# A mixture-of-experts kernel: an expert's last tile of at most 64 tokens in 32-column groups

## The chip, the cores and the metric

The kernel runs on one core of a Trainium2 chip. The metric is device time in microseconds of one execution. A core has five engines with instruction queues of their own: TensorE (PE) multiplies matrices into PSUM, VectorE (DVE) and ScalarE (ACT) read PSUM and work elementwise, GpSimd (POOL) issues the indirect DMAs here, and SyncE (SP) issues nearly all other DMAs. [...]

## What is computed

x has 4 sequences of 512 tokens with 256 features. The reference adds two layers to it, each on top of a small conditioned layer:

```python
x = x + attn(cond(x, cond_8))            # attention, 16 heads of 16 features, keys and values shared
x = x + ffn(cond2(x, cond_8))            # the mixture of experts, 8 experts

# in ffn: 8 groups of 256 tokens
probs = softmax(xg @ w_router)           # over 8 experts
_, idx = top_k(probs, 2)                 # two experts for each token
# at most 128 tokens of a group are kept for one expert
h = gelu(expert_in @ wi[e])              # 256 -> 1024
expert_out = h @ wo[e]                   # 1024 -> 256
out = sum over the two experts of expert_out * probs
```

All is float32. How many tokens an expert gets depends on the data and is known only on the chip.

## The kernel before

The first 380 us or so are the conditioned layer and the attention, with the routing of each finished sequence worked in beside it. The matter here is the last part, the experts.

**Rows by expert.** Every routed token row (256 features and 8 extra numbers: token number, first expert, two shares) is scattered by an indirect DMA (L654) into a DRAM buffer `xp`, where each expert has a range of 1024 rows and its rows lie without gaps. Behind the last row of an expert lie zero rows.

**Units.** The experts' work is cut into units. A double unit is 256 rows of one expert, a single is 128 rows. Unit numbers stand for slots of lists: NA = 6 doubles that are listed early, from the first sequences; NB = 5 doubles from all rows; then NTILE slots for singles, everything that is left. `list_of` (L835) computes on VectorE, for each slot, its expert (`texp`, and the weights' row in `table`) and its first row (`table`). It is called for the early doubles, then in `lists_of_rest` (L877) for the later doubles and for the singles, in this order; `count` (L887) holds the number of singles. Slots past the end of a list point to zero rows. A partly filled single costs what a full one does.

**A unit's steps.** `fetch_in` and `fetch_out` (L901, L907) read a row number from `table` into a register of SP and load 1 MB each of the expert's weights wi and wo (L896); the tiles have three buffers each. `fetch_rows` (L913) loads the rows (L918, four buffers). `turn` (L954) transposes the rows on TensorE (L960; four transposes for a double, two for a single) and VectorE copies them to SBUF (L962). `up` (L964) multiplies with wi: for each of 8 blocks of 128 hidden features two matmuls (L975) with a 128 x 128 block of wi as the stationary operand and the unit's 128 or 256 tokens moving; ScalarE applies Gelu from PSUM (L979). `put` (L1001) multiplies with wo for each 128 tokens: 8 matmuls with 128 tokens stationary and 256 output features moving (L1005). `share` (L986) finds each row's weight and target on VectorE (L994 to L998), VectorE scales the result into `y` (L1015), POOL casts the target row (L1013) and issues an indirect DMA that adds `y` to the output (L1016). The adds of a unit wait for the adds of the unit before, because the same rows may be hit.

**The order** is written out by hand in `run` (L1107), without a scheduler. Step k: load the rows of unit k+2; `up` of unit k; load wi for k+3; `turn` of unit k+1; `put` of unit k-1; load wo for k+2. `place` (between these steps) puts in what is left of the last sequence's attention and routing; its twelfth entry is `lists_of_rest`. Units run in this order: the 6 early doubles, NSURE = 14 singles, the 5 later doubles. Then `count` is loaded, and only if it is over 14 do further singles run in a branch.

Parts used below: an f32 matmul shows as two records in the trace. The attention weighs values in `weigh` (L421): four matmuls, each with 32 stationary columns, write the four groups of 32 partitions of one PSUM bank.

Of the kernel before, what the change touches and what calls it, by code (L numbers as in the profile page):

```python
# [10 lines left out]
F32 = mybir.dt.float32  # L11
I32 = mybir.dt.int32
AF = mybir.ActivationFunctionType
ALU = mybir.AluOpType
# [8 lines left out]
NE = 8  # L23
# [7 lines left out]
NCH = NT // P  # L31
EROWS = NG * CAP
NTILE = 2 * NCH + NE - 1


N0, NA, NB, NSURE, NNEXT = 2, 6, 5, 14, 18
XROW = D + NE
WROW = 1024 + 10

# [2 lines left out]
def adaln_attn_ffn_kernel(  # L42
# [32 lines left out]
    def bank(tag):  # L75
        return ps.tile([P, 512], F32, tag=tag, name=f"ps_{tag}", bufs=BANKS[tag])
# [731 lines left out]

    NUNIT = NA + NB + NTILE
    pairs = fp.tile([P, NE + 1], F32, name="pairs", bufs=1)
    nc.gpsimd.memset(pairs, 0.0)
    texp = fp.tile([P, NUNIT], F32, name="texp", bufs=1)
# [3 lines left out]
    def of_experts(t, less, op, begin):  # L818

        n = begin.shape[2]  # L820
        cmp = fp.tile([P, NE, NG], F32, name="cmp", bufs=1)[:, :, 0:n]
        nc.vector.scalar_tensor_tensor(
            cmp, free.unsqueeze(2).to_broadcast([P, NE, n]), less, begin, ALU.add, op
        )
        nc.vector.tensor_reduce(t, cmp, AX.X, ALU.add)

    def ends_of_experts(t):

        cmp = fp.tile([P, NE, NE], F32, name="cmp2", bufs=1)
        nc.vector.tensor_tensor(cmp, through, t.unsqueeze(1).to_broadcast([P, NE, NE]), ALU.mult)  # L830
        end = fp.tile([P, NE], F32, name="end", bufs=1)
        nc.vector.tensor_reduce(end, cmp, AX.X, ALU.add)
        return end

    def list_of(u0, n, got, end, used, width):  # L835


        step = fp.tile([P, NE], F32, name="step", bufs=1)
        nc.vector.tensor_tensor(step, used[:, 1 : NE + 1], used[:, 0:NE], ALU.subtract)
        nc.vector.tensor_tensor(step, step, got, ALU.subtract)  # L840
        nc.vector.tensor_scalar(step, step, float(EROWS // (width * P)), None, ALU.add)
        past = fp.tile([P, NTILE, NE], F32, name="past", bufs=1)[:, 0:n]
        nc.vector.tensor_tensor(
            past, tilen[:, 0:n].unsqueeze(2).to_broadcast([P, n, NE]),
            end.unsqueeze(1).to_broadcast([P, n, NE]), ALU.is_ge,
        )
        te = texp[:, u0 : u0 + n]
        nc.vector.tensor_reduce(te, past, AX.X, ALU.add)
        nc.vector.tensor_scalar(
            table[:, 1, u0 : u0 + n], te, float(NE - 1), 4.0 * P, ALU.min, ALU.mult  # L850
        )
        nc.vector.tensor_tensor(past, past, step.unsqueeze(1).to_broadcast([P, n, NE]), ALU.mult)
        row = fp.tile([P, NTILE], F32, name="trow", bufs=1)[:, 0:n]
        nc.vector.tensor_reduce(row, past, AX.X, ALU.add)
        nc.vector.scalar_tensor_tensor(row, row, used[:, 0:1], tilen[:, 0:n], ALU.add, ALU.add)
        nc.vector.tensor_scalar(
            table[:, 0, u0 : u0 + n], row, float(NE * EROWS // (width * P)), float(width * P),
            ALU.min, ALU.mult,
        )
# [17 lines left out]
    def lists_of_rest():  # L877
        for _ in list_of_pairs(NA, NB):
            pass
        got = fp.tile([P, NE], F32, name="got", bufs=1)  # L880
        twice = fp.tile([P, NE + 1], F32, name="twice", bufs=1)
        nc.vector.tensor_scalar(twice, pairs, 2.0, None, ALU.mult)
        of_experts(got, 0.0, ALU.is_gt, begin)
        nc.vector.tensor_tensor(got, got, twice[:, 0:NE], ALU.subtract)
        end = ends_of_experts(got)
        list_of(NA + NB, NTILE, got, end, twice, 1)
        nc.vector.tensor_copy(count, end[:, NE - 1 : NE])  # L887

    wi_of, wo_of, xt_of, xT_of, hT_of = {}, {}, {}, {}, {}
    reg, adds, now = {}, [], []  # L890
# [1 line left out]
    def width(u):  # L892
        return 2 if u < NA + NB else 1
# [60 lines left out]
    def turn(u, tag="a"):  # L954
# [6 lines left out]
        xT_of[u] = fp.tile([P, 2, 2 * P], F32, name="xT")[:, :, 0 : w * P]  # L961
        nc.vector.tensor_copy(xT_of[u], pt)  # L962

    def up(u, half):  # L964

        n = width(u) * P
        if half == 0:
            t = ep.tile([P, 4, 4, P], F32, name="e").rearrange("p a b t -> p (a b t)")
            hT_of[u] = t[:, 0 : F // P * n].rearrange("p (f t) -> p f t", f=F // P)
        each = 512 // n  # L970
        for f0 in range(4 * half, 4 * half + 4, each):
            ph = bank("m")
            for k in range(each):
                for c in range(2):
                    mm(  # L975
                        ph[:, ts(k, n)], wi_of[u][:, c, ts(f0 + k, P)], xT_of[u][:, c, :],
                        start=c == 0, stop=c == 1,
                    )
            nc.scalar.activation(  # L979
                hT_of[u][:, f0 : f0 + each].rearrange("p f t -> p (f t)"), ph,  # L980
                AF.Gelu_apprx_tanh,
            )
# [17 lines left out]

    def put(u, h):  # L1001

        po = bank("x")
        for fc in range(F // P):
            mm(  # L1005
                po[:, 0:D], hT_of[u][:, fc, ts(h, P)], wo_of[u][:, fc, :],
                start=fc == 0, stop=fc == F // P - 1,
            )
        if h == 0:
            share(u)  # L1010
        w0, at = shares[u]
        to = fp.tile([P, 1], I32, name="to_row", bufs=6)
        nc.gpsimd.tensor_copy(to, at[:, h : h + 1])  # L1013
        y = fp.tile([P, D], F32, name="y", bufs=6)
        nc.vector.tensor_scalar(y, po[:, 0:D], w0[:, h : h + 1], None, ALU.mult)  # L1015
        i = nc.gpsimd.indirect_dma_start(  # L1016
            out=out_rows,
            out_offset=bass.IndirectOffsetOnAxis(ap=to, axis=0),
            in_=y,
            in_offset=None,  # L1020
            compute_op=ALU.add,
        )


        for k in adds[-1] if adds else ():
            tc.add_manual_dep(i.ins, k.ins.name, AFTER, reason="same rows")
        if h > 0:
            tc.declare_no_dep(i.ins, group=f"unit{u}", reason="other tokens")
        tc.add_to_no_dep_group(f"unit{u}", i.ins)
        if u < NA:  # L1030
            tc.declare_no_dep(i.ins, group="last rows", reason="other sequences")
            tc.add_to_no_dep_group("early adds", i.ins)
        elif u == first_of_rest[0] and h == 0:
            for k in last_rows:
                tc.add_manual_dep(i.ins, k.ins.name, AFTER, reason="rows of the last sequence")
        now.append(i)
        if h == width(u) - 1:
            adds.append(list(now))
            now.clear()
# [46 lines left out]
    def place():  # L1086

        for name in final.get(next(places), ()):
            if name == "rest":
                lists_of_rest()  # L1090
                ready.update(range(NA, NUNIT))
                for f, u in late:
                    f(u)
                late.clear()
            else:
                work[B - 1][name]()
# [10 lines left out]
    def run(units, rows, begun=False):  # L1107

        if not begun:
            turn(units[0])  # L1110
        for k in range(len(units) + 1):
            for u in units[k : k + 1]:
                for x in rows(k):
                    fetch_rows(units[x])
                if begun and k == 0:
                    turn(units[1], "x")
                else:
                    up(u, 0)
                if width(u) == 2:
                    place()  # L1120
                up(u, 1)
                for x in units[k + 3 : k + 4]:
                    fetch(fetch_in, x)
                for x in units[k + 1 : k + 2]:
                    if not begun or k > 0:
                        turn(x)
                place()
            for u in units[k - 1 : k] if k else ():
                for h in range(width(u)):
                    put(u, h)  # L1130
                    place()
            for x in units[k + 2 : k + 3]:
                fetch(fetch_out, x)

    singles = range(NA + NB, NUNIT)
    units = [*range(NA), *singles[:NSURE], *range(NA, NA + NB)]

    def rows_behind(k):
        return (k + 2,) if k + 2 < len(units) else ()

    run(units, rows_behind, begun=True)
    filled = nc.values_load(count[0:1, 0:1], min_val=0, max_val=NTILE)

    def more(units):
        for u in units[:3]:
            fetch_in(u)
            fetch_out(u)
        for u in units[:2]:
            fetch_rows(u)
        run(units, lambda k: range(k + 2, len(units))[:1])  # L1150

    with tc.If(filled > NSURE):
        more(singles[NSURE:NNEXT])
        with tc.If(filled > NNEXT):
            more(singles[NNEXT:])


# [78 lines left out]
```

## Time and profile before

| | |
|---|---|
| three runs | 663.63 us median (662.09 to 665.27) |
| the profiled execution | 663.3 us, its span 661.6 us, mean granted clock 0.991 |
| TensorE busy | 642.0 us |
| VectorE, ScalarE, GpSimd busy | 324.2, 226.0, 111.6 us |
| DMA | 107.46 MB, mean 162 GB/s |
| first up of an expert unit, last down | 380.4 us, 647.9 us |
| matmul records of up (L975), down (L1005) | 800, 576 |
| row adds (L1016) | 36, 6.2 us from issue to landing |

The span runs from the first to the last instruction; the device time has 1.7 us more. The page gives each engine's busy time, the chain of waits that ended last, and the costliest groups of instructions: line, engine, operation, output and inputs, partitions x elements, count, busy time, mean duration. In the timeline a line holds start, duration, engine, line, operation and how many records were merged; in brackets the idle time before it and what ended it. Matmuls overlap, so the distance of two starts tells more than a duration.

### The profile page before, as it was taken

The page shows a single profiled execution, that of the slowest core. Times are in us where ns is not written, and L with a number is a line of the kernel's source. Part 1 is how long each engine was busy: PE and PEld are TensorE (multiplying, and loading weights), DVE is VectorE, ACT ScalarE, POOL GpSimd, SP SyncE. Part 2 cuts the span into 40 slices and gives each one's busy share as a digit, 9 for nine tenths or more (in the row PEclk, how much of TensorE's full clock was granted, in tenths as well). Part 3 has the DMA queues.
Part 4 walks back from the last instruction along what each step waited for, and adds up shares of the span by engine and source line. Part 5 has one row for each costly group of instructions (what it writes and reads, how often), then busy time and mean ns, then how long its engine had stood idle before and what let it go on. Part 6 is the DMA issues. An engine that isn't in the chain of part 4 may idle for free.

```text
span 661.6 us, 10602 instructions
## 1 busy us (share of the span) xinstructions
PE 642.0 (97%) x3988; PEld 393.3 (59%) x3988; DVE 324.2 (49%) x782; ACT 226.0 (34%) x400; POOL 111.6 (17%) x146
## 2 busy tenths in 40 slices
PE   8999999999999999999999899999999999999991
PEld 3444454333334433343344388888999999988881
DVE  1184745577667687867887625472122222221210
ACT  1122123566665465546545631311012111121110
POOL 1600000000000000400040402245322222222231
PEclk9999999999999999999999899999999999999997
DMA  7943971200232114320144399429899999974411
GB/s 234 371 137 95 317 224 49 81 33 18 63 99 84 34 33 131 132 65 17 46 139 152 102 390 273 138 83 297 238 297 303 340 334 319 348 224 121 88 18 26
DMA packets 65724, 107.46 MB, mean 162 GB/s; under 512 B 6914, under 2 KB 27266, under 8 KB 65666
## 3 DMA queue, kind: packets, MB, share of 16 engines
q1 hardware_dynamic: 50066, 87.96, 40.3%
q0 software_dynamic: 6720, 9.05, 7.2%
q10 hardware_dynamic: 8880, 9.71, 4.7%
q8 instruction: 33, 0.54, 0.3%
q14 instruction: 25, 0.20, 0.1%
HBM read 79.59 MB, written 26.98 MB: 161 GB/s over the span
## 4 chain that ended last, share of the span: by engine, by line
PE 88%; DMA 6%; DVE 3%; issue 1%; SPq 1%; POOL 0%; POOLq 0%; DVEq 0%
PE ps_m L374 19%; PE ps_x L1005 17%; PE ps_m L975 16%; PE ps_a L421 10%; PE ps_x L262 4%; PE ps_a L278 4%; PE ps_x L280 4%; PE ps_x L533 2%; PE ps_x L312 2%; PE ps_x L403 2%; PE ps_x L501 2%; DMA wo_sb<-in_wo_dram 2%; DMA inv<-od 1%; PE ps_x L327 1%; PE ps_a L960 1%
## 5 line engine op out<-in xcount | busy, mean ns | idle before, releaser
L378 DVE TENSOR_REDUCE negm<-ps_m 128x1 f32<-128x512 f32 x250 | 160.5, 684 | 64.9 <-PE ps_x L403 43.8
L407 ACT ACTIVATE e<-ps_x 128x512 f32<-128x512 f32 x244 | 132.4, 594 | 107.9 <-PE ps_x L403 101.4
L374 PE MATMUL ps_m<-k,q 32*128 32x512 f32 x500 | 152.3, 639 | 0.4 <-DVE negm L378 0.4
L403 PE MATMUL ps_x<-q,k 32*128 32x512 f32 x488 | 139.6, 642 | 1.9 <-DMA q<-nmT 1.9
L975 PE MATMUL ps_m<-xT,wi_sb 128*128 128x128 f32 (+1 forms) x800 | 130.3, 321 | 0.0
L1005 PE MATMUL ps_x<-wo_sb,e 128*128 128x256 f32 x576 | 128.5, 379 | 0.0
L975 PEld LDWEIGHTS ps_m<-xT,wi_sb 128*128 128x128 f32 x800 | 118.9, 191 | 10.1 <-issue 0.4
L1005 PEld LDWEIGHTS ps_x<-wo_sb,e 128*128 128x128 f32 x576 | 107.6, 190 | 13.7
L979 ACT ACTIVATE e<-ps_m 128x512 f32<-128x512 f32 x72 | 42.8, 597 | 194.3 <-PE ps_m L975 192.8
L374 PEld LDWEIGHTS ps_m<-k,q 32*128 32x128 f32 x500 | 46.5, 183 | 55.7 <-DVE negm L378 25.4
L1016 POOL DMA_INDIRECT out_dram<-y,to_row x36 | 56.1, 1558 | 131.6 <-DVE y L1015 33.2
L421 PE MATMUL ps_a<-e,v 128*32 128x256 f32 x1024 | 76.6, 392 | 0.1
L421 PEld LDWEIGHTS ps_a<-e,v 128*32 128x32 f32 x1024 | 23.3, 109 | 80.2 <-issue 66.5
L962 DVE COPY xT<-ps_a 128x256 f32<-128x256 f32 (+1 forms) x23 | 12.2, 529 | 95.1 <-PE ps_a L960 95.1
L1015 DVE TENSOR_SCALAR y<-ps_x,w 128x256 f32<-128x256 f32 x36 | 17.4, 482 | 81.5 <-PE ps_x L1005 81.5
L654 POOL DMA_INDIRECT xp<-x,to_i x32 | 32.9, 1028 | 53.7 <-DVE negm L378 28.8
L403 PEld LDWEIGHTS ps_x<-q,k 32*128 32x128 f32 x488 | 38.2, 184 | 4.4 <-issue 4.2
L583 POOL TENSOR_SCALAR x<-mk 128x4 f32<-128x4 f32 x4 | 0.8, 196 | 208.0 <-DVE mk L580 208.0
L283 DVE SCALAR_TENSOR_TENSOR hid<-ps_x,wo_sb,sg 128x512 f32<-128x512 f32 x16 | 12.0, 749 | 45.5 <-PE ps_x L280 45.5
L278 PE MATMUL ps_a<-xT_sb,wi_sb 128*128 128x512 f32 x64 | 30.5, 599 | 0.3 <-DMA wi_sb<-in_wcond_dram 0.3
L280 PE MATMUL ps_x<-xT_sb,wi_sb 128*128 128x512 f32 x64 | 30.1, 592 | 0.0
L1013 POOL CAST to_row<-at 128x1 int32<-128x1 f32 x36 | 20.1, 558 | 55.1 <-DVE at L998 55.1
(150 smaller groups left out, 436.9 us busy)
## 6 DMA issues: line engine op xcount, KB each, us to landing
wi_sb<-in_wi_dram SPq DMA_DIRECT2D x25, 1024.0 KB
wo_sb<-in_wo_dram SPq DMA_DIRECT2D x25, 1024.0 KB
xp<-zeros ACTq DMA_DIRECT2D x1, 8712.0 KB
q<-qd SPq DMA_DIRECT2D x8, 512.0 KB
wi_sb<-in_wcond_dram SPq DMA_DIRECT2D x15, 256.0 KB
od<-stage SPq DMA_DIRECT2D x15, 256.0 KB
xt<-xp SPq DMA_DIRECT2D x11, 264.0 KB
wo_sb<-in_wcond_dram SPq DMA_DIRECT2D x4, 517.0 KB
```

What stands on the lines that cost most here:

```text
L278: mm(pu, wu[:, c, :], xT_sb[:, c, ts(b, T)], start=c == 0, stop=c == 1)
L280: mm(pg, wg[:, c, :], xT_sb[:, c, ts(b, T)], start=c == 0, stop=c == 1)
L374: mm(pm, q[32 * j : 32 * j + 32, i, ts(hg, P)], k[32 * j : 32 * j + 32, :], start=True, stop=True,)
L378: nc.vector.tensor_reduce(nm[:, i, j : j + 1], pm, AX.X, ALU.max, negate=True)
L403: mm(px, k[rows_j, ts(sc, P)], seqs[u // 4]["q"][rows_j, :, ts(u % 4, P)], start=True, stop=True,)
L407: nc.scalar.activation(e_of[n][:, :, j, :].rearrange("p h (i t) -> p i h t", i=4), px.rearrange("p (i h t) -> p i h t", i=4, h=4), AF.Exp,)
L421: i = mm(pa_of[u][32 * hh : 32 * hh + 32, j0 * P : (j0 + nj) * P], seqs[b]["v"][:, sc, :], e[:, hh, j0 : j0 + nj].rearrange("p j n -> p (j ...
L654: i = nc.gpsimd.indirect_dma_start(out=xp, out_offset=bass.IndirectOffsetOnAxis(ap=s["to_i"][:, k, ch : ch + 1], axis=0), in_=s["x3"][:, c ...
L975: mm(ph[:, ts(k, n)], wi_of[u][:, c, ts(f0 + k, P)], xT_of[u][:, c, :], start=c == 0, stop=c == 1,)
L979: nc.scalar.activation(hT_of[u][:, f0 : f0 + each].rearrange("p f t -> p (f t)"), ph, AF.Gelu_apprx_tanh,)
L1005: mm(po[:, 0:D], hT_of[u][:, fc, ts(h, P)], wo_of[u][:, fc, :], start=fc == 0, stop=fc == F // P - 1,)
L1016: i = nc.gpsimd.indirect_dma_start(out=out_rows, out_offset=bass.IndirectOffsetOnAxis(ap=to, axis=0), in_=y, in_offset=None, compute_op=AL ...
```

## The change

`lists_of_rest` now makes two lists of what the doubles leave: tiles with more than 64 rows (slots as before) and, behind them, one slot per expert for a last tile of 1 to 64 rows. NSURE goes from 14 to 10, and NSMALL = 4 slots of the new list run without a branch. `count` becomes the largest excess of the two lists over 10 and 4; if it is over 0, the branch runs further units of both kinds.

A small unit takes the same row load, `turn`, two weight loads and row add. In between it differs. `up_small` makes 32 tokens the stationary operand and 512 columns of wi the moving one: four matmuls (two halves of the 64 tokens, two halves of the 1024 hidden features) write the four groups of 32 partitions of one bank, twice for the 256 input features; one Gelu follows. `turn_small` transposes the 128 x 512 result in four blocks, and VectorE copies it. `put_small` makes 16 matmuls with 32 stationary columns and 256 moving ones; two partition groups hold the sum of one half of the hidden features, two that of the other. ScalarE copies one half out of PSUM, VectorE adds the other, and scales. 64 rows are added to the output.

In the order, a small unit's `turn_small` stands after the `put` of the unit before it. The 5 later doubles and the 4 small units alternate, beginning and ending with a double.

```diff
-N0, NA, NB, NSURE, NNEXT = 2, 6, 5, 14, 18
+HALF = 64
+N0, NA, NB, NSURE, NNEXT, NSMALL = 2, 6, 5, 10, 18, 4
...
-    NUNIT = NA + NB + NTILE
+    NUNIT = NA + NB + NTILE + NE
...
-        of_experts(got, 0.0, ALU.is_gt, begin)
-        nc.vector.tensor_tensor(got, got, twice[:, 0:NE], ALU.subtract)
-        end = ends_of_experts(got)
-        list_of(NA + NB, NTILE, got, end, twice, 1)
-        nc.vector.tensor_copy(count, end[:, NE - 1 : NE])
+        most = fp.tile([P, 1], F32, name="most", bufs=1)
+        nc.vector.memset(most, 0.0)
+        for u0, n, less, sure in (
+            (NA + NB, NTILE, -float(HALF), NSURE), (NA + NB + NTILE, NE, 0.0, NSMALL)
+        ):
+            of_experts(got, less, ALU.is_gt, begin)
+            nc.vector.tensor_tensor(got, got, twice[:, 0:NE], ALU.subtract)
+            end = ends_of_experts(got)
+            list_of(u0, n, got, end, twice, 1)
+            nc.vector.tensor_tensor(twice[:, 0:NE], twice[:, 0:NE], got, ALU.add)
+            nc.vector.scalar_tensor_tensor(
+                most, end[:, NE - 1 : NE], -float(sure), most, ALU.add, ALU.max
+            )
+        nc.vector.tensor_copy(count, most)
...
+    def up_small(u):
+        t = ep.tile([P, 4, 4, P], F32, name="e").rearrange("p a b t -> p (a b t)")
+        hT_of[u] = t
+        ph = bank("m")
+        for c in range(2):
+            for n in range(4):
+                mm(
+                    ph[32 * n : 32 * n + 32, :], xT_of[u][:, c, ts(n % 2, 32)],
+                    wi_of[u][:, c, ts(n // 2, 512)], start=c == 0, stop=c == 1,
+                )
+        nc.scalar.activation(t[:, 0:512], ph, AF.Gelu_apprx_tanh)
+
+    def turn_small(u):
+        t = hT_of[u]
+        pt = bank("x")
+        for k in range(4):
+            nc.tensor.transpose(pt[:, ts(k, P)], t[:, ts(k, P)], ident)
+        nc.vector.tensor_copy(t[:, 512:1024], pt)
+
+    def put_small(u):
+        hT = hT_of[u][:, 512:1024].rearrange("p (k t) -> p k t", k=4)
+        po = bank("x")
+        for k in range(4):
+            for n in range(4):
+                mm(
+                    po[32 * n : 32 * n + 32, 0:D], hT[:, k, ts(n, 32)],
+                    wo_of[u][:, 4 * (n // 2) + k, :], start=k == 0, stop=k == 3,
+                )
+        share(u)
...
+        nc.scalar.copy(half, po[HALF:P, 0:D])
+        nc.vector.tensor_tensor(y[0:HALF], po[0:HALF, 0:D], half, ALU.add)
+        nc.vector.tensor_scalar(y[0:HALF], y[0:HALF], w0[0:HALF], None, ALU.mult)
+        add(u, to[0:HALF], y[0:HALF], 0)
...
+            for u in units[k : k + 1]:
+                if is_small(u):
+                    turn_small(u)
...
-    units = [*range(NA), *singles[:NSURE], *range(NA, NA + NB)]
+    units = [*range(NA), *singles[:NSURE]]
+    for n in range(max(NB, NSMALL)):
+        units += [*range(NA, NA + NB)[n : n + 1], *small[:NSMALL][n : n + 1]]
...
-    with tc.If(filled > NSURE):
-        more(singles[NSURE:NNEXT])
+    with tc.If(left > 0):
+        more([*singles[NSURE:NNEXT], *small[NSMALL:]])
```

More of the change, by code (lines that the diff above doesn't have):

```diff
@@ L962, in turn, with is_small @@
         nc.vector.tensor_copy(xT_of[u], pt)
+    def is_small(u):
+        return u >= NA + NB + NTILE
+    def up_small(u):
[25 more added lines that the diff above has]
+        share(u)
+        w0, at = shares[u]
+        to = fp.tile([P, 1], I32, name="to_row", bufs=6)
+        nc.gpsimd.tensor_copy(to, at[:, 0:1])
+        y = fp.tile([P, D], F32, name="y", bufs=6)
+        half = fp.tile([HALF, D], F32, name="half", bufs=2)
+        nc.scalar.copy(half, po[HALF:P, 0:D])
+        nc.vector.tensor_tensor(y[0:HALF], po[0:HALF, 0:D], half, ALU.add)
+        nc.vector.tensor_scalar(y[0:HALF], y[0:HALF], w0[0:HALF], None, ALU.mult)
+        add(u, to[0:HALF], y[0:HALF], 0)
     def up(u, half):
+        if is_small(u):
+            if half == 0:
+                up_small(u)
+            return
         n = width(u) * P
@@ L1001, in put @@
     def put(u, h):
+        if is_small(u):
+            put_small(u)
+            return
         po = bank("x")
@@ L1015, in put, with add @@
         nc.vector.tensor_scalar(y, po[:, 0:D], w0[:, h : h + 1], None, ALU.mult)
+        add(u, to, y, h)
+    def add(u, to, y, h):
         i = nc.gpsimd.indirect_dma_start(
@@ L1131, in run @@
                     place()
+            for u in units[k : k + 1]:
+                if is_small(u):
+                    turn_small(u)
             for x in units[k + 2 : k + 3]:
                 fetch(fetch_out, x)
-    singles = range(NA + NB, NUNIT)
-    units = [*range(NA), *singles[:NSURE], *range(NA, NA + NB)]
+    singles = range(NA + NB, NA + NB + NTILE)
+    small = range(NA + NB + NTILE, NUNIT)
+    units = [*range(NA), *singles[:NSURE]]
+    for n in range(max(NB, NSMALL)):
+        units += [*range(NA, NA + NB)[n : n + 1], *small[:NSMALL][n : n + 1]]
     def rows_behind(k):
@@ L1141, in adaln_attn_ffn_kernel @@
     run(units, rows_behind, begun=True)
-    filled = nc.values_load(count[0:1, 0:1], min_val=0, max_val=NTILE)
+    left = nc.values_load(count[0:1, 0:1], min_val=0, max_val=NTILE)
     def more(units):
@@ L1150, in more @@
         run(units, lambda k: range(k + 2, len(units))[:1])
-    with tc.If(filled > NSURE):
-        more(singles[NSURE:NNEXT])
-        with tc.If(filled > NNEXT):
+    with tc.If(left > 0):
+        more([*singles[NSURE:NNEXT], *small[NSMALL:]])
+        with tc.If(left > NNEXT - NSURE):
             more(singles[NNEXT:])
```

## Prediction

> **What bounds the kernel now.** I read the page first, then the chain of waits in order of time, then the stages, then the TensorE timeline. The page says whose work the span is:
>
> ```profile
> PE 642.0 (97%) x3988; PEld 393.3 (59%) x3988; DVE 324.2 (49%) x782; ACT 226.0 (34%) x400; POOL 111.6 (17%) x146
> ...
> PE 88%; DMA 6%; DVE 3%; issue 1%; SPq 1%; POOL 0%; POOLq 0%; DVEq 0%
> ```
>
> TensorE is busy for 97% and 88% of the chain is its work. The chain shows the stretch that the change touches:
>
> ```profile
> 454.89 6.91 PE ps_m L975 x32
> ...
> 552.08 3.57 PE ps_m L975 x32
> 555.87 3.46 PE ps_x L1005 x16
> 559.32 3.57 PE ps_m L975 x32
> 563.11 3.46 PE ps_x L1005 x16
> 566.57 3.57 PE ps_m L975 x32
> 570.57 3.46 PE ps_x L1005 x16
> 574.03 6.91 PE ps_m L975 x32
> ```
>
> From 454.89 on every step is TensorE: up (L975) and down (L1005) of one unit after another. Singles follow each other every 7.24 us (559.32 less 552.08): up 3.57, turning the next rows 0.22, down 3.46. A double takes twice that. So an instruction taken out of this stretch shortens the span one for one, as long as no other wait ends later. The stages, asked for by window (columns: PE, PEld, DVE, ACT and POOL busy us, clock, DMA share, GB/s):
>
> ```profile
> 469.00:566.00 97.00, 97.00 (x665) 91.27 (x664) 22.59 (x92) 15.53 (x26) 24.05 (x28) 1.00 0.99 310
> 574.00:648.00 74.00, 74.00 (x353) 65.08 (x351) 12.91 (x45) 11.95 (x20) 18.26 (x22) 1.00 0.49 126
> ```
>
> Both are full on TensorE at full clock. Beside the singles the DMA engines are 99% busy with weights, beside the last doubles only 49%. No matmul there waits for a load, so that fullness hides, but it is close.
>
> **What the skill says.** The Trainium skill, TensorEngine Tiling (Array Packing), Tiling Modes, has four independent tiles of 128 rows by 32 columns, and says that changing the mode drains the engine. The same page, Performance Considerations, warns that PSUM evacuation isn't sped up. The trace before has such groups of four in the attention (L421):
>
> ```profile
> 378.33 1.17 PE L403 MATMUL ps_m<-q,k 32*128 32x512 f32 x3
> 379.43 1.07 PE L421 MATMUL ps_a<-e,v 128*32 128x256 f32 x16
> 380.43 3.72 PE L975 MATMUL ps_m<-xT,wi_sb 128*128 128x256 f32 x16
> ```
>
> (the same lines at other places: eight records, at 359.49, are followed at 360.06.) An f32 matmul is two records. Sixteen records are two groups of four matmuls of 256 columns, and take 1.00 us to the next instruction; eight take 0.57, so a group of four costs 0.43 us, what one full-width matmul of 256 columns costs (L1005: 3.46 us for 8). Four do run side by side for the price of one, and entering and leaving the mode costs 1.00 - 2 x 0.43 = 0.14 us plus some at entry: around 384 us the starts of single matmuls stand 0.31 apart going in, 0.24 after the first four, 0.31 going out and 0.17 after the first transpose, where 0.22 (0.11 for the transpose) is usual. That is 0.27 in all. TensorE: Matmul & The Clock Gate, Part 3, gives three column tiles at 512 columns only 2.38x; the trace has no column group of 512. The row groups of four at 512 (L403) pass at 0.52 to 0.53 us per four records where 0.43 would be no loss. I keep that as the dear end.
>
> **How many tiles.** The reference's routing, run on its own inputs, keeps 598, 537, 464, 660, 623, 478, 307 and 428 tokens for the eight experts: 36 tiles of 128. Eleven doubles take 22, which leaves 14 singles; the page's 36 row adds (L1016) are 2 x 11 + 14, and agree. The last tiles hold 86, 25, 80, 20, 111, 94, 51 and 44: four are of at most 64. So the new lists have 10 and 4, just the sizes run without a branch, and the nearest to 64 is 13 tokens off.
>
> **The change, part by part.**
>
> 1. *Four singles leave*: 4 x 7.24 = 28.98 us of TensorE off the path.
>
> 2. *Four small units come.* Up: 8 matmuls of 32 x 512, two groups of four, each twice the columns of L421's: 2 x 0.86 = 1.73 us (dear end 4 x 0.53 = 2.1). Turning the hidden rows: 4 transposes; a double's turn is 4 and takes 0.44 (0.22 for a single's two). Down: 16 matmuls of 32 x 256, four groups, 4 x 0.43 = 1.73. The turn of its own rows stays, 0.22. Sum 4.12, times four 16.5. A small unit's down is followed directly by the next one's up, both in the narrow mode, so there are five stretches in that mode, not eight: 5 x 0.27 = 1.3. In all 17.8 us, and the saving is 28.98 - 17.8 = **11.1 us** (9.5 with the dear end, 12 if mode changes cost nothing).
>
> 3. *What hides the new dependencies.* The small up's Gelu (0.60, L979) and the turn after it: between lie the next turn and both downs of the double before, 7.3 us. The copy of the turned rows (128 x 512 from PSUM, 0.69 as L962): under the next double's up, 6.91. The two PSUM reads after the down (ScalarE copy, about 0.40 between its 0.23 for 32 and 0.60 for 512 columns; VectorE add 0.43 as L537) lie beside the next up. Were this cover gone, each would cost some 1 us per unit. ScalarE's table stays, since its copy at 415 us loaded none. Cost on the path 0.
>
> 4. *The second list.* About 20 more VectorE instructions at some 0.2 us, 4.1 us, in the place where the tables are made. Queued behind them on VectorE are:
>
> ```profile
> 446.38 0.47 DVE L1015 TENSOR_SCALAR y<-ps_x,w 128x256 f32<-128x256 f32 x1
> 448.02 0.69 DVE L962 COPY xT<-ps_a 128x512 f32<-128x512 f32 x1 [1.17 <-PE ps_a L960]
> ```
>
> TensorE wants that xT at 454.89; its copy now ends at 448.7 and would end near 451.7, 3.2 us ahead. The loads for the first single wait for the singles' own list, made before the small one, so they move by 0.1 to 0.5 us; its rows wait longer anyway, until 453.96, for the scatters. Cost 0; 1 at most.
>
> 5. *Moved*: the four units' loads (rows, two of 1 MB each) go from the singles' run to between the doubles, on SP behind each double's last down. A double and a small unit take 14.25 + 4.4 = 18.7 us and move two times 2.1 MB, some 0.4 MB of rows and 0.3 MB of adds: 4.9 MB, 262 GB/s, under the 310 seen. Each load keeps two units of lead, 10 us or more. Its row add goes through POOL in the same order. Cost 0.
>
> 6. *The end.* The last double's first add waits for the landing of the unit before:
>
> ```profile
> 641.44 0.48 DVE L1015 TENSOR_SCALAR y<-ps_x,w 128x256 f32<-128x256 f32 x1 [2.97 <-PE ps_x L1005]
> ...
> 642.69 1.56 POOL L1016 DMA_INDIRECT out_dram<-y,to_row  x1 [1.71 <-DVE w L997]
> ...
> 647.24 1.55 POOL L1016 DMA_INDIRECT out_dram<-y,to_row  x1 [2.79 <-DMA out_dram<-y,to_row]
> ...
> 649.60 1.56 POOL L1016 DMA_INDIRECT out_dram<-y,to_row  x1 [0.61 <-POOL to_row L1013]
> ```
>
> The unit before is now small, and its row result comes by copy, add and product, 1.3 us after its down instead of 0.5. That moves its add, hence the next, by 0.8 us at most; an add of 64 rows may land sooner. Bounds 0 and 0.85; I take 0.5.
>
> Sum against the profiled run's own 663.3 us (span 661.6 and 1.7 around it): 663.3 - 11.1 + 0.5 = 652.7. That run is 0.3 below the median of those shown, so **653.0 us**.
>
> **Rivals.** *Loads become the bound* between doubles: if they ran at 250 GB/s (the page's slices around 463 us have 297 and 238), 4.9 MB would take 19.6 us against 18.7, a wait of 0.9 for each of four: 656.5 with little lead used. For it: the 99% share beside the singles. Against it: 49% beside the doubles, and three buffers of lead. *The add chain at the end* counts more: if landing and POOL's serial issue slip by 2 us more, 655. *The groups don't run side by side* at 512 columns, or where two of the four read the same weights: this is the case on the other side. A small unit costs 0.93 plus 3.46 times the factor by which a group is longer than one matmul; it equals 7.24 at a factor of 1.82. Two at a time gives 7.85, or 666; one at a time 14.8, or 693. Against it stands L421. *The change doesn't do what it says*: if the lists came out longer than 10 and 4, the branch would run eight slots of single and four of small size with cold weights, over 75 us: 730 or more. Against it, the counts above.
>
> **Chances.** Forecast 0.80 (its own range 651 to 655), loads 0.07, add chain 0.07, no side by side 0.04 (half of it near 666), lists 0.02. A measurement can tell about 0.5% (3.3 us) from no change: faster 0.94, same 0.02, slower 0.04. The range, 651 to 656.5, takes in the cheap mode change, the dear 512-column groups and both mild rivals.
>
> **What would show it.** Between the doubles, matmuls of 128*32 128x512 in fours 0.43 us apart; each small up and down near 1.75 us; doubles still at 6.91 and 6.91; singles still 7.24 apart, ten of them; no TensorE idle from 455 us on; the last down ending near 637.2. Wrong would be: fours 0.8 us apart or more, TensorE waiting for wi_sb or wo_sb, a wait for xT near 455, or more than 36 row adds.

## The result and the profile after

The changed kernel took 652.4 us (median of 4, 651.4 to 653.11) against 663.05 (662.09 to 665.27): a ratio of 0.9834, 95% interval 0.9804 to 0.9863. The forecast was 653.0. The profiled run took 652.6, its span 650.9.

The page, first engines, then the chain's shares:

```profile
PE 630.8 (97%) x4004; PEld 373.9 (57%) x4004; DVE 330.4 (51%) x810; ACT 225.1 (35%) x400; POOL 111.9 (17%) x146
...
PE 87%; DMA 6%; DVE 3%; issue 1%; POOL 1%; SPq 0%; ACT 0%; POOLq 0%
```

TensorE lost 11.2 us of work and is as full as before. VectorE gained 6 us and nothing came of it: it isn't what ends last. The chain, at the end of the singles:

```profile
455.25 6.91 PE ps_m L1035 x32
...
530.69 3.57 PE ps_m L1035 x32
534.48 3.46 PE ps_x L1068 x16
537.94 3.57 PE ps_m L1035 x32
541.95 3.46 PE ps_x L1068 x16
545.40 6.91 PE ps_m L1035 x32
552.53 3.46 PE ps_x L1068 x16
555.98 1.85 PE ps_m L985 x16
558.42 6.91 PE ps_x L1068 x32
565.77 6.91 PE ps_m L1035 x32
572.90 1.86 PE ps_x L1005 x32
574.76 1.72 PE ps_m L985 x16
577.07 6.91 PE ps_x L1068 x32
584.41 6.91 PE ps_m L1035 x32
```

(L1035 and L1068 are now up and down, L985 and L1005 those of a small unit.) Singles still stand 7.25 apart. Two doubles with a small unit between them stand 584.41 - 565.77 = 18.64 us apart, a double alone was 14.25, so a small unit costs 4.39 us where a single cost 7.24. The timeline of TensorE shows the parts: down of one small unit (L1005), then up of the next (L985), between two turns of rows (L971):

```profile
572.52 0.38 PE L971 MATMUL ps_a<-ident,xt 128*128 128x128 f32 x2
572.83 1.93 PE L1005 MATMUL ps_x<-wo_sb,e 128*32 128x256 f32 x32
574.58 1.90 PE L985 MATMUL ps_m<-wi_sb,xT 128*32 128x512 f32 x16
576.41 0.66 PE L971 MATMUL ps_a<-ident,xt 128*128 128x128 f32 x4
```

Down takes 1.75 us from start to start, up 1.83. In up the records start in fours 0.43 us apart (574.58, 575.01, 575.44, 575.87), as single full-width records of 512 columns do elsewhere in this trace. The stages, with the columns as before (PE, PEld, DVE, ACT, POOL, clock, DMA share, GB/s):

```profile
470.00:545.00 75.00, 75.00 (x511) 70.51 (x510) 17.31 (x70) 11.95 (x20) 18.58 (x22) 1.00 0.99 307
545.00:638.00 93.00, 92.57 (x570) 73.29 (x568) 23.83 (x82) 15.81 (x28) 26.34 (x32) 1.00 0.69 203
```

The DMA engines' share beside the doubles rose from 0.49 to 0.69, since the small units' weights now come there, and TensorE waits for none of it. The place on VectorE where the second list is made:

```profile
450.14 0.47 DVE L1078 TENSOR_SCALAR y<-ps_x,w 128x256 f32<-128x256 f32 x1
450.53 0.68 DVE L973 COPY xT<-ps_a 128x512 f32<-128x512 f32 x1
```

The copy that TensorE needs at 455.25 ends at 451.21, 2.5 us later than before and still 4.0 ahead. And the end:

```profile
630.40 7.17 PE L1068 MATMUL ps_x<-wo_sb,e 128*128 128x256 f32 x32
...
632.48 1.44 POOL L1082 DMA_INDIRECT out_dram<-y,to_row  x1 [8.16 <-DVE w L1057]
...
636.43 1.56 POOL L1082 DMA_INDIRECT out_dram<-y,to_row  x1 [2.30 <-DMA out_dram<-y,to_row]
...
638.86 1.56 POOL L1082 DMA_INDIRECT out_dram<-y,to_row  x1 [0.66 <-POOL to_row L1076]
```

The last row add is issued 1.29 us after the last matmul's end (637.57), as before (649.60 less 648.31). The trace puts its wait down to `to_row`, but that ended 0.61 us ahead before and 0.66 after, while `y` (L1078), which hangs on the last down, ended 0.77 us ahead in both.

### The profile page after: what moved, and what is told of

The parts are those of the page before. It is cut to its first block, busy times and chain, and to the rows that moved or that the text cites. A ratio compares the mean times of both kernels' runs of the same rounds, so it can differ in the third digit from the quotient of the medians.

```text
span 650.9 us, 10666 instructions
## 1 busy us (share of the span) xinstructions
PE 630.8 (97%) x4004; PEld 373.9 (57%) x4004; DVE 330.4 (51%) x810; ACT 225.1 (35%) x400; POOL 111.9 (17%) x146
## 4 chain that ended last, share of the span: by engine, by line
PE 87%; DMA 6%; DVE 3%; issue 1%; POOL 1%; SPq 0%; ACT 0%; POOLq 0%
PE ps_m L375 19%; PE ps_x L1068 15%; PE ps_m L1035 15%; PE ps_a L422 9%; PE ps_a L279 4%; PE ps_x L263 4%; PE ps_x L281 4%; PE ps_x L534 2%; PE ps_x L313 2%; PE ps_x L404 2%; PE ps_x L502 2%; DMA wo_sb<-in_wo_dram 2%; DMA inv<-ivd 2%; DMA inv<-od 1%; PE ps_x L1005 1%; PE ps_x L328 1%
## 5 line engine op out<-in xcount | busy, mean ns | idle before, releaser
L1035 PE MATMUL ps_m<-xT,wi_sb 128*128 128x256 f32 (+1 forms) x672 | 115.4, 330 | 0.0
L1068 PE MATMUL ps_x<-wo_sb,e 128*128 128x256 f32 x512 | 114.3, 379 | 0.0
L1035 PEld LDWEIGHTS ps_m<-xT,wi_sb 128*128 128x128 f32 x672 | 103.7, 191 | 9.7 <-issue 0.4
L1068 PEld LDWEIGHTS ps_x<-wo_sb,e 128*128 128x128 f32 x512 | 95.6, 190 | 12.6 <-issue 0.4
L1039 ACT ACTIVATE e<-ps_m 128x512 f32<-128x512 f32 x64 | 38.0, 597 | 175.6 <-PE ps_m L1035 174.0
L1078 DVE TENSOR_SCALAR y<-ps_x,w 128x256 f32<-128x256 f32 x32 | 15.4, 482 | 63.9 <-PE ps_x L1068 63.9
L263 PE MATMUL ps_x<-hid,wo_sb 128*128 128x512 f32 x64 | 28.8, 597 | 0.0
```

The costliest lines, as they stand in the source:

```text
L263: mm(po, wd[:, hc, ts(dc, P)], hid_of[b][:, hc, :], start=hc == 0, stop=hc == 3)
L1035: mm(ph[:, ts(k, n)], wi_of[u][:, c, ts(f0 + k, P)], xT_of[u][:, c, :], start=c == 0, stop=c == 1,)
L1039: nc.scalar.activation(hT_of[u][:, f0 : f0 + each].rearrange("p f t -> p (f t)"), ph, AF.Gelu_apprx_tanh,)
L1068: mm(po[:, 0:D], hT_of[u][:, fc, ts(h, P)], wo_of[u][:, fc, :], start=fc == 0, stop=fc == F // P - 1,)
```

## The experiments

My theory: the gain is TensorE work, four small units at 4.4 us for four singles at 7.24, and all else that the change does is hidden. Rivals: the order brings it (loads moved to where the DMA engines are half idle); the narrow groups matter as such, not the columns that stream; the list, the loads or the dependencies are hidden only just, or not for the reason given. The kernel before took 663.05, 665.63, 663.67 and 665.44 us (medians) in the four groups of runs, so each run is compared by its ratio to the kernel before in its own group; in two of the three groups below, the changed kernel ran there too.

**The changed kernel again.** 

> The changed kernel once more, as the yardstick for the other runs of this chip. Expected 652.4 us, within 1 us.


It took 654.08 us against 665.63 (ratio 0.9839, 0.9806 to 0.9871): both kernels are some 2 us slower here, at nearly the same ratio. 

> The changed kernel once more, beside the next runs on the same chip: 1.6% under the kernel before.


It took 654.39 us against 665.44, 0.9834 (0.981 to 0.9858).

**List and order without small units.**

```diff
     def is_small(u):
-        return u >= NA + NB + NTILE
+        return False
```

> The second list, the new order and the branch stay, but the four last tiles are computed as ordinary singles of 128 tokens. If the whole gain is TensorE work, the time is that of the kernel before, 663 us, within 1 us. If the order (loads spread between the doubles, where the DMA engines are idle half the time) or the shorter list brings part of it, the time is under 661; if the second list costs something on the path, over 664.


665.8 us against 665.63, ratio 1.0006 (0.9996 to 1.0016). List, order and branch together are worth nothing by themselves, from 0.3 us of gain to 1.1 of loss. The rival that the order brings the gain is out.

**Two groups of 64.**

```diff
-            for n in range(4):
-                mm(ph[32 * n : 32 * n + 32, :], xT_of[u][:, c, ts(n % 2, 32)],
-                    wi_of[u][:, c, ts(n // 2, 512)], ...)
+            for n in range(2):
+                mm(ph[64 * n : 64 * n + 64, :], xT_of[u][:, c, 0:HALF],
+                    wi_of[u][:, c, ts(n, 512)], ...)
```

(down likewise) 

> Two groups of 64 columns side by side instead of four of 32: half as many matmuls in up and down (4 and 8), same layout of the results. If the cost is only the number of columns that stream through, it is the same: 2 pairs x 0.86 us up, 4 pairs x 0.43 us down, 652.4 us within 0.7. If it takes groups of 32 columns to run side by side, pairs go one after the other and each of the four units costs 3.5 us more: 666 us.


654.6 us, ratio 0.9842 (0.9816 to 0.9869); the changed kernel beside it 654.08. The timeline has half the records and the same times:

```profile
573.70 1.95 PE L1005 MATMUL ps_x<-wo_sb,e 128*64 128x256 f32 x16
575.47 1.89 PE L985 MATMUL ps_m<-wi_sb,xT 128*64 128x512 f32 x8
577.29 0.66 PE L971 MATMUL ps_a<-ident,xt 128*128 128x128 f32 x4
```

1.77 and 1.82 us. What is paid is the columns that stream past, with all 128 columns of the array in use: the 32 in the change's name is not what matters for 64 tokens.

**The same matmuls, group by group.**

```diff
-        for k in range(4):
-            for n in range(4):
+        for n in range(4):
+            for k in range(4):
                 mm(po[32 * n : 32 * n + 32, 0:D], hT[:, k, ts(n, 32)], ...)
```

(up likewise) 

> The same matmuls, but issued group by group: all of group 0, then all of group 1, and so on, in up and in down. If starts are strictly in order, a matmul waits for the one before it in its own group, and only the edges of neighbouring groups overlap: up takes 5 x 0.86 = 4.3 us instead of 1.73, down 13 x 0.43 = 5.6 instead of 1.73, so each unit costs 6.5 us more and the kernel 678 us, slower than before. If each group has a queue of its own, nothing changes: 652.4 us.


665.28 us, ratio 0.9994 (0.9979 to 1.0009): neither 678 nor 652.4. The whole gain is gone, 11.2 us, 2.8 per unit, not the 6.5 of strict order and not zero. The timeline tells which half:

```profile
557.70 1.95 PE L985 MATMUL ps_m<-wi_sb,xT 128*32 128x512 f32 x16
559.57 0.66 PE L971 MATMUL ps_a<-ident,xt 128*128 128x128 f32 x4
...
574.63 3.95 PE L1005 MATMUL ps_x<-wo_sb,e 128*32 128x256 f32 x29
578.20 0.64 PE L985 MATMUL ps_m<-wi_sb,xT 128*32 128x512 f32 x3
578.41 0.59 PE L1005 MATMUL ps_x<-wo_sb,e 128*32 128x256 f32 x2
```

Up by itself is unharmed (the first small unit's takes 1.87 us to the next instruction); down grew from 1.75 to 3.57, and an up right behind it from 1.83 to 2.67, since its last group has to wait for the last group of down. From 574.63 to the turn after the next up, at 580.87, it is 6.24 us, against 3.58 in the changed kernel. In up a group has 2 matmuls, four records; in down 4, eight records. The starts of single records in this stretch: group 0 starts at 574.630, 574.870, 575.086, 575.302 and 575.518, and only then, at 575.524, does group 1 begin; its fifth is at 576.411, and group 2 begins at 576.417. So a new theory: issue is in order, a group holds about four records (one running, three waiting), and the ninth record, the first of the next group, can leave only when the eighth has found room.

**Down, two matmuls of a group at a time.**

```diff
-        for k in range(4):
+        for k0 in (0, 2):
             for n in range(4):
+                for k in (k0, k0 + 1):
-                mm(po[32 * n : 32 * n + 32, 0:D], hT[:, k, ts(n, 32)], ...)
+                    mm(po[32 * n : 32 * n + 32, 0:D], hT[:, k, ts(n, 32)], ...)
```

> Down is issued two matmuls of a group at a time (four records), then two of the next group, and after the fourth group the other two of each. From the starts of the run issued group by group: issue is in order, and each group of columns holds about four records, since the next group's first started just as the fifth of eight started. If so, chunks of four records fit, all four groups start at once, and the time is that of the changed kernel within 1 us. If the loss grows with the length of a chunk whatever the holding, a chunk of two matmuls costs about a third of the 11 us that four cost, 3 to 4 us.


654.67 us, ratio 0.9838 (0.9813 to 0.9863), beside 654.39 for the changed kernel. Down is back at 1.75 us:

```profile
574.82 1.97 PE L1006 MATMUL ps_x<-wo_sb,e 128*32 128x256 f32 x32
576.57 1.94 PE L985 MATMUL ps_m<-wi_sb,xT 128*32 128x512 f32 x16
```

Chunks of four records cost nothing, chunks of eight the whole gain. That a group holds four fits both runs; chunks of six were not tried, and what in the engine holds the four is not shown.

**Small units in a row.**

```diff
-    for n in range(max(NB, NSMALL)):
-        units += [*range(NA, NA + NB)[n : n + 1], *small[:NSMALL][n : n + 1]]
+    units += [*small[:NSMALL], *range(NA, NA + NB)]
```

> The four small units stand one after the other behind the ten singles, before the five doubles. TensorE would need 4.4 us for each, but each needs 2.1 MB of weights and 0.2 MB of rows and adds, about 7 us at the 310 to 340 GB/s seen beside the singles. If loads become the bound there, as one rival had it, part of the gain goes: 655 to 661 us, with TensorE waiting for wi_sb or wo_sb. If three buffers of lead are enough, 652.4 us.


658.26 us against 663.67, ratio 0.9915 (0.9887 to 0.9943): about 5 us of the gain are lost. TensorE does wait, but for the rows:

```profile
554.65 0.41 PE L971 MATMUL ps_a<-ident,xt 128*128 128x128 f32 x2 [0.28 <-DMA xt<-xp]
...
561.03 0.41 PE L971 MATMUL ps_a<-ident,xt 128*128 128x128 f32 x2 [1.66 <-DMA xt<-xp]
...
567.75 0.63 PE L971 MATMUL ps_a<-ident,xt 128*128 128x128 f32 x4 [2.01 <-DMA xt<-xp]
```

The first two turns are of small units (132 KB of rows), the third is of a double (264 KB). The DMA engines are full there:

```profile
545.00:580.00 35.00, 31.05 (x278) 18.52 (x276) 12.65 (x42) 5.88 (x11) 7.24 (x9) 1.00 1.03 350
```

The two loads of 1 MB have three buffers of lead. The rows are asked for only one step ahead of their turn, each 1.2 us behind a load of 1 MB; those of the double took 9.4 us from issue (558.18) to landing. That it is the weights ahead of them that hold them up is argued from this order, not tested. So the place between the doubles is needed: not for a gain of its own (the run without small units shows none) but to keep this one.

**Only up in groups.**

```diff
-        for k in range(4):
-            for n in range(4):
+        for n in range(2):
+            for k in range(4):
                 mm(
-                    po[32 * n : 32 * n + 32, 0:D], hT[:, k, ts(n, 32)],
-                    wo_of[u][:, 4 * (n // 2) + k, :], start=k == 0, stop=k == 3,
+                    po[0:HALF, 0:D], hT[:, k, ts(n, HALF)], wo_of[u][:, 4 * n + k, :],
+                    start=(n, k) == (0, 0), stop=(n, k) == (1, 3),
...
-        nc.scalar.copy(half, po[HALF:P, 0:D])
-        nc.vector.tensor_tensor(y[0:HALF], po[0:HALF, 0:D], half, ALU.add)
...
```

> Only up runs in groups side by side; down multiplies 64 tokens at a time, 8 matmuls of 256 columns one after the other, as many as an ordinary single has, into one group of partitions (so the copy and the addition of the two halves go). If the sum of TensorE work is right, each unit costs 3.46 instead of 1.73 us in down: 4 x 1.73 = 6.9 more, 659.3 us.


659.55 us against 663.67, ratio 0.9946 (0.9928 to 0.9964). The changed kernel didn't run in this group; its ratio of 0.9839 would be 653.0 us here, so this is 6.5 us more. Down takes 575.94 - 572.35 = 3.59 us:

```profile
572.35 3.67 PE L1005 MATMUL ps_x<-wo_sb,e 128*64 128x256 f32 x16
575.94 1.92 PE L985 MATMUL ps_m<-wi_sb,xT 128*32 128x512 f32 x16
```

Sixteen records of 64 columns one after the other cost about what sixteen of 128 cost (3.46); only a neighbour at work makes the narrow one cheap.

**The hidden rows turned at once.**

```diff
             if half == 0:
                 up_small(u)
+                turn_small(u)
...
-            for u in units[k : k + 1]:
-                if is_small(u):
-                    turn_small(u)
```

> The four transposes of the hidden rows stand right behind up, before the down of the double, so nothing covers the Gelu. TensorE waits for it, about 0.60 us and 0.2 of signals for each unit: 4 x 0.8 = 3.2 us more, 655.6 us. If the wait is hidden in the queue anyway, 652.4 us.


655.35 us against 663.67, ratio 0.9885 (0.9856 to 0.9913), 2.3 us over the 653.0. The interval overlaps the changed kernel's (0.9806 to 0.9871), so the times alone hardly settle it; the trace does, since each of the four units shows the wait:

```profile
554.71 1.92 PE L985 MATMUL ps_m<-wi_sb,xT 128*32 128x512 f32 x16
557.41 0.66 PE L996 MATMUL ps_x<-ident,e 128*128 128x128 f32 x4 [0.78 <-ACT e L989]
```

The cover of the Gelu is the down of the double before it, and it is worth 0.77 us per unit in the trace.

**The small list three times.**

```diff
+            for _ in range(2 if n == NE else 0):
+                of_experts(got, less, ALU.is_gt, begin)
+                nc.vector.tensor_tensor(got, got, twice[:, 0:NE], ALU.subtract)
+                list_of(u0, n, got, ends_of_experts(got), twice, 1)
```

> The small list is computed three times over, two more passes of about 3.2 us on VectorE. The copy of the next rows ends at 451.2 us after the change and TensorE asks for it at 455.3: 4.1 us of slack. If that slack is what hides the list, two more passes overrun it by some 2.3 us: 654.7 us, with TensorE waiting for xT. If something else hides it or the list is not on any path, 652.4 us; if all of the list is on the path, 658.8 us.


655.79 us against 663.67, ratio 0.9888 (0.986 to 0.9916), 2.8 us over 653.0, again with overlapping intervals. The trace is plain: TensorE stands still once, from 455.0 on, and goes on 0.1 us after the copy of xT ends (456.81 + 0.68):

```profile
447.96 7.07 PE L1072 MATMUL ps_x<-wo_sb,e 128*128 128x256 f32 x32
457.59 7.15 PE L1039 MATMUL ps_m<-xT,wi_sb 128*128 128x256 f32 x32 [2.56 <-issue]
```

One pass takes 3.17 us (446.89 to 450.06). The slack of some 4 us hides one list, not three.

**Two units of 32 tokens.**

```diff
+        if is_tiny(u):
+            for c in range(2):
+                for n in range(4):
+                    mm(ph[32 * n : 32 * n + 32, 0:256], xT_of[u][:, c, 0:32],
+                        wi_of[u][:, c, ts(n, 256)], ...)
```

(`is_tiny` holds for slots 0 and 1; two transposes, 8 matmuls down, one more copy and addition) 

> The first two small slots hold 25 and 20 tokens with these inputs. They are computed with one group of 32 tokens: the four groups of columns take a quarter of the hidden features each (4 x 2 matmuls of 256 columns up, two transposes, 8 matmuls of 256 down, and one more copy and addition to sum four parts). The list doesn't test for it, so this kernel is right for such inputs only, as a bound. If what is paid is the columns that stream, each of the two saves 0.86 up, 0.22 and 0.86 down: 3.9 us under the changed kernel. If a short burst is ruled by its mode changes and loads, under 2 us.


650.41 us against 665.44, ratio 0.9771 (0.9746 to 0.9796): 4.0 us under the changed kernel beside it (654.39). Down and up of two such units:

```profile
573.43 1.07 PE L1018 MATMUL ps_x<-wo_sb,e 128*32 128x256 f32 x16
574.32 1.05 PE L989 MATMUL ps_m<-wi_sb,xT 128*32 128x256 f32 x16
575.30 0.66 PE L971 MATMUL ps_a<-ident,xt 128*128 128x128 f32 x4
```

0.89 and 0.98 us from start to start. So paying by the columns that stream goes on to a quarter. It is the fastest kernel here, but it leaves out the test that a tile has at most 32 rows; a third list with that test would make it right for all inputs, and was not tried.

**One slot too few.**

```diff
-N0, NA, NB, NSURE, NNEXT, NSMALL = 2, 6, 5, 10, 18, 4
+N0, NA, NB, NSURE, NNEXT, NSMALL = 2, 6, 5, 10, 18, 3
```

> Only three small slots run without the branch, so the list of four overflows it: the branch runs 8 empty single slots and 5 small slots, of which one is full. The price of the rival in which the lists don't fit: 4.4 us less in the straight part, 8 x 7.24 + 5 x about 7 (weights for small units in a row) more, and a start with cold weights: 740 us, 715 to 760.


752.3 us (two runs) against 665.44, ratio 1.1304 (1.1251 to 1.1358). The chain runs through the branch's eight single slots (7.25 us each), then through two loads of rows for its small units, 7.01 and 9.02 us from issue to landing. The rival of lists that don't fit has its price, about 98 us over the changed kernel, and did not happen: these inputs fill 10 and 4 slots exactly.

## Why the prediction was right, step by step

1. *Four singles, 28.98 us, leave.* Held: the singles that stay are 7.25 us apart (and 28.98 is four times 7.245, the mean distance before).

2. *17.8 us come in.* Held: 4 x 4.39 = 17.6 from the distance of two doubles, which leaves out the fifth stretch in the narrow mode. From TensorE at 455 us to its last end it was 648.31 - 454.89 = 193.42 before and is 637.57 - 455.25 = 182.32: 11.10 us less, and 11.1 was forecast; so 28.98 - 11.10 = 17.9 came in. (The bound for mode changes that cost nothing should have read 28.98 - 16.5 = 12.5, not 12.) The doubtful term, groups at 512 columns, came at the cheap end: 1.83 us for up with the way out of the mode. Fours of 512 columns start 0.43 us apart, as one full-width record does, so four column groups run at four times the rate; neither the 2.38x that the Trainium skill (TensorE: Matmul & The Clock Gate, Part 3) has for three column tiles nor the 0.53 of the row groups applied. Whether the groups run side by side was a rival of the prediction; it turned out to hang on the order of issue, which the prediction didn't name: issued group by group, the same matmuls lost the whole gain.

3. *The dependencies cost nothing.* Held. For the Gelu the cover is what was named: taking it away cost 0.77 us per unit, where the prediction had some 1. The covers of the other two, the copy of the turned rows and the two PSUM reads, were not taken away.

4. *The second list costs nothing.* Held. It ran to 450.1, some 3.4 us rather than 4.1, so the slack is 4.0 instead of 3.2 (0.36 of it because TensorE itself comes that much later); the run with three lists overran it.

5. *The moved loads cost nothing.* Held between the doubles (share 0.69). But "two units of lead" is right for the weights only: the rows have one step, 9.8 us at the least between the doubles (asked for at 566.57, turned at 576.41). The rival of loads was right on the mechanism where there is no cover, as the run in a row shows, but named the wrong tile: xt, not wi_sb or wo_sb.

6. *The end costs 0.5.* The term was too dear: 0. The small unit's add was indeed issued later after its down (632.48 - 630.47 = 2.0 us instead of 642.69 - 641.40 = 1.3). But it held the next add for only 3.95 us (to 636.43) instead of 4.55 (whether because it adds 64 rows isn't shown), and the last add waits for the last down either way.

What is left of the difference, 10.7 us of span instead of 11.1, lies ahead of the change: the chain passes the attention's normalising at 339.54 instead of 339.16 behind a landing of `inv<-ivd`, in a part that the edit doesn't touch. I take it for scatter between executions; that wasn't tested. This 0.4 and the 0.5 of the end offset each other in the total, and that is luck.

## What to carry to other kernels

On a stretch where TensorE is full, a tile that fills half of the stationary side pays for the whole. Making the few tokens stationary and sending the weights through several column groups side by side brings the cost of up and down to the tokens that are there: a half at 64 tokens, in groups of 32 or of 64 columns alike, and a quarter at 32. Issue the groups in turn: runs of four f32 matmuls for one group made the others wait and cost the whole gain, runs of two cost nothing, and three were not tried. A unit that became shorter needs its weights and, above all, its rows just as soon as a long one, so put it between long ones, and put the steps that it waits for, such as the Gelu, under their matmuls.

## What was not expected of the hardware

- Two runs fit the theory that a column group holds about four records and that issue stops at the first that finds no room. Eight records in a row for one group left only two groups at work at a time (3.57 us for 32 records until the next up began, instead of 1.75).
- A matmul issued later may start before an earlier one of another group: in the run issued group by group the next up began at 578.204, while group 3 still had three records of down to start (578.414, 578.630, 578.845).
- Sixteen records with 64 stationary columns took 3.59 us alone and, in pairs, 1.77.
- Loads of rows, issued a step ahead but behind weights with the DMA engines full, made TensorE wait up to 1.7 us (132 KB) and 2.0 us (264 KB).
